# Layer 2 of a four-layer network: the order of a turn's links, and one product instruction for each half

## The chip, the cores and the metric

The kernel runs on one core of a Trainium2 chip. What counts is the device time of one launch in microseconds. A core has five engines that each work through their own queue in order: TensorE (PE in the profile), VectorE (DVE), ScalarE (ACT), GpSimd (POOL) and SyncE (SP), which here issues every DMA. They wait for each other through semaphores.

## The reference

A batch of 16 images of 64 x 64 pixels and 256 channels, all float32, goes through four residual layers. Each computes `x = x + layer(group_norm(x))`. Cut to what matters:

```python
def _gn(v, G=32, eps=1e-5):        # mean and variance over all pixels and the 8 channels of a group
    ...
# layer 0: linear attention, ends in a norm over channels
x = x + _L0_conv_ref(_gn(x), ...)
# layer 1: channel gate, a scan and a 7x7 gate, batch norm, relu
x = x + _L1_conv_ref(_gn(x), ...)
# layer 2: involution 3x3
x = x + _L2_conv_ref(_gn(x), ...)
# layer 3: involution 7x7
x = x + _L3_conv_ref(_gn(x), ...)

def _L2_conv_ref(x, Wr, br, gamma, beta, mean, var, Ws, bs, Wi, bi):
    r = relu(((x @ Wr + br) - mean) * rsqrt(var + 1e-3) * gamma + beta)
    w = (r @ Ws + bs).reshape(B, H, W, 16, 9)[:, :, :, :, None, :]   # 9 factors for each of 16 groups
    xi = x @ Wi + bi
    patches = stack(the 9 shifted copies of xi, padded).reshape(B, H, W, 16, 16, 9)
    return sum(w * patches, -1).reshape(B, H, W, 256)
```

Note the last reshape: the nine shifted copies of 256 channels stand one behind the other as 2304 numbers, which are cut into 256 runs of nine. So an output channel is a sum over nine neighbours in that row of 2304, each multiplied by a factor.

## The kernel before

The program has stages, one behind the other: layer 0 with the statistics for layer 1; a short stage for the scan and the gates; one long loop for the end of layer 1, all of layer 2, and the preparation of layer 3; then layer 3. The change lies in the long loop, in `for n in range(TURNS)`. Its order is written out by hand (`tc.manual_schedule()`): each engine gets its instructions in the order of the text.

**A turn** handles 512 pixels (8 rows, one `rc`; eight turns make an image) of up to four jobs at once, which are `LAG` turns apart, so that each works on an older chunk:

- *the end of layer 1* (`end_of_layer1`, lag 0), in three parts that the loop starts with `next(ending)`. First, on VectorE, two links that scale the loaded x1: `z` and `pf` (L975; the second is written over its own factor, so the profile calls it pf). Then, on ScalarE, the relu of both (L981) and, on GpSimd, the sums with x1 that make x2 (L985). Last, on ScalarE, the squares of x2 for the group norm of layer 2 (L992).
- *the projection of layer 2* (`projected`, lag 12): TensorE multiplies x2 by `Wi` (px, L1038) and ScalarE writes it into the padded image `pad` (L1042).
- *the involution* (lag 20). One turn ahead, `prepare` makes r (pr and rt, L1059 and L1062), the transposed patches `xs` (36 transposes L1084 into nine PSUM tiles pt, nine copies L1088 by ScalarE) and the factors `pw` (L1069). In the turn itself, `residual` transposes x2 into the PSUM tiles `lo`, one for each half of 128 output channels (L1100). `products` multiplies patches by factors on VectorE (pd, L1107), four instructions of 1152 elements for each half. The nine products of an output are summed for half 0 on GpSimd (`sums_on_pool`, L1122 and L1123) and for half 1 on VectorE (a reduce, L1258). The residual `lo` is added to each half on VectorE (L1261, half 1 first). The result x3 is held in `made`; in the next turn `turned` transposes it back (L1135) and ScalarE evicts it as c3 (L1136) with the sums for the group norm of layer 3, and `statistics3` squares it (L1156).
- *the centring for layer 3* (`centred`, lag 30): GpSimd subtracts the group means from x3, loaded again as `xc`, into `cen` (L880), and twelve stores write it as `strips`.

**Norm links.** The group norms are generators with small instructions on 128 x 2 elements. `begun` starts them with a fill (L113 to L123); `step()` moves every running one on by a link: a matmul (L134), a copy (L140), a deviation of three instructions (L146 to L148), a second matmul (L151), the inverse square root (L93, L94). `step()` stands three times in a turn: behind `turned`, behind the products, and at the end behind the residual. Each image has two such norms, for layers 2 and 3.

**DMAs.** SP issues all of them in the order of the text. A turn begins with the loads for the next one (x2p, x2r, x1 as two, pf as two), then come the stores that the turn before left in `stores`, in the order in which its jobs put them there (L1215), then the four loads of xc. Each is issued with one of eight semaphores, taken in turn.

**Buffers.** The PSUM pool `tr` has three tiles that pr, pt, px and the norms' matmuls share in turn; `pw` has three, `lo` two (one a half). In SBUF, xs, pd, x1, x2, c3, xc and cen have two each, x2r and x3 three.

Of the kernel before, what the change touches and what calls it, by code (L numbers as in the profile page):

```python
# [11 lines left out]
ALU = mybir.AluOpType  # L12
# [3 lines left out]
P = 128  # L16
C = 256
# [19 lines left out]
def network(ctx: ExitStack, tc: tile.TileContext, a: dict, out: bass.AP):  # L37
    nc = tc.nc
# [59 lines left out]
    def step():  # L98

        for c in list(chains):  # L100
            if next(c, c) is c:
                chains.remove(c)
# [77 lines left out]
    with ExitStack() as st:  # L180
# [366 lines left out]
        def loads(n):  # L547
            for job in jobs(n):
                if job[0] == "q":
                    load("xn", job[1], job[3])  # L550
                else:
                    load(*job)
# [78 lines left out]
    with ExitStack() as st:  # L631
# [57 lines left out]
        for n in range(10):  # L689
            delta, c = n // 2, n % 2  # L690
# [28 lines left out]
        with tc.manual_schedule():  # L719
# [25 lines left out]
            for n, (ch, g) in enumerate(steps):  # L745
# [18 lines left out]
                b, k = g * 8, min(8, NI - g * 8)  # L764
# [134 lines left out]
    with ExitStack() as st:  # L899
# [45 lines left out]
        def taken(name):  # L945

            n = [k for k, _ in loaded].index(name)
            return loaded.pop(n)[1]
# [11 lines left out]
        def load_centred(i, rc):  # L960
            load("xc", [P, 4, C], *(
                (lambda t, k=k: t[:, k], src) for k, src in enumerate(centred_from(i, rc))
            ))

        def end_of_layer1(i, rc):

            if rc == 0:
                st0[i] = [
                    wk.tile([P, 2, NCH], F32, tag=f"st0{k}", name="st0") for k in range(2)
                ]  # L970
            sums, squares = st0[i]
            x1, pf = taken("x1"), taken("pf")
            zs = [wk.tile([P, 2, 256], F32, tag="z", name="z", bufs=1), pf]
            for h, z in enumerate(zs):
                nc.vector.scalar_tensor_tensor(  # L975
                    z, x1[:, h], ngm1[:, i, h : h + 1], pf, ALU.add, ALU.mult
                )
            yield
            x2 = wk.tile([P, 2, CT], F32, tag="x2", name="x2")
            for h, z in enumerate(zs):  # L980
                nc.scalar.activation(  # L981
                    z, z, AF.Relu, bias=bnp[:, 1, h : h + 1], scale=ab[:, 0, i, h : h + 1],
                    accum_out=sums[:, h, rc : rc + 1],
                )
                nc.gpsimd.tensor_tensor(  # L985
                    x2[:, h].rearrange("p (t g) -> p g t", g=2), z, x1[:, h], ALU.add
                )
            stores.append((x2_d[i, rc], x2))
            yield
            sq = wk.tile([P, CT], F32, tag="sq", name="sq", bufs=1)  # L990
            for h in range(2):
                nc.scalar.activation(  # L992
                    sq, x2[:, h], AF.Square,
                    bias=ngm1[:, i, h : h + 1], accum_out=squares[:, h, rc : rc + 1],
                )
            if rc == NCH - 1:
                begun.append(norm2(i))
# [104 lines left out]

        def products(oh, pw, xs):
            pd = pd_p.tile([P, 4, P, 9], F32, tag="pd", name="pd")
            for r in range(4):
                run = xs[:, r : r + 3].rearrange("p e j c -> p (e j c)")
                nc.vector.tensor_tensor(  # L1107
                    pd[:, r].rearrange("p (g f) k -> p g f k", f=16),
                    run[:, oh * 9 * P : (oh + 1) * 9 * P].rearrange(
                        "p (g f k) -> p g f k", f=16, k=9  # L1110
                    ),
                    pw[:, r].rearrange("p (g k) -> p g k", k=9).unsqueeze(2).broadcast_to(
                        [P, 8, 16, 9]
                    ),
                    ALU.mult,
                )
            return pd

        def sums_on_pool(pd, x3):
# [5 lines left out]
        def turned(i, rc, x3):  # L1125

            if rc == 0:
                st3[i] = [
                    wk.tile([P, 2, NCH], F32, tag=f"st3{k}", name="st3") for k in range(2)
                ]  # L1130
            c3 = wk.tile([P, 2, 2, 256], F32, tag="c3", name="c3", bufs=2)
            for oh in range(2):
                pt = tr.tile([P, 4, P], F32, tag="tr", name="pt")
                for r in range(4):
                    nc.tensor.transpose(pt[:, r, :], x3[:, r, oh * P : (oh + 1) * P], ident)  # L1135
                nc.scalar.activation(  # L1136
                    c3[:, oh], pt.rearrange("p r t -> p (r t)").rearrange("p (t g) -> p g t", g=2),
                    AF.Copy, accum_out=st3[i][0][:, oh, rc : rc + 1],
                )
            x3n = x3_d[i].rearrange("(g r w) c -> g w r c", g=2, w=HW)  # L1140
            for g in range(2):
                stores.append((x3n[g][:, rc * 4 : rc * 4 + 4], x3[g:P:2]))
            for h in range(2):
                stores.append((
                    c3_d[i, :, h].rearrange("p (g t) -> p g t", g=2)[
                        :, :, rc * 256 : rc * 256 + 256
                    ],
                    c3[:, h],
                ))
            return c3  # L1150
# [23 lines left out]
        def centred(i, rc):  # L1174
            cen = wk.tile([P, 4, 4, 64], F32, tag="cen", name="cen")
            stores.extend(centred_strips(i, rc, taken("xc"), cen, gmb[i]))
# [6 lines left out]

        LAG = (0, 12, 20, 30)
        TURNS = NI * NCH + 23

        def jobs(n):

            at = [divmod(n - lag, NCH) for lag in LAG]
            return [
# [13 lines left out]
        with tc.manual_schedule():  # L1206
            loads(0)
            ahead, made = None, None
            for n in range(TURNS):
                end, proj, inv, cen = jobs(n)  # L1210
                nxt = jobs(n + 1)[2]
                done, stores[:] = list(stores), []
                loads(n + 1)
                for dst, src in done:
                    nc.sync.dma_start(out=dst, in_=src)  # L1215
                nxt_cen = jobs(n + 1)[3]
                if nxt_cen:
                    load_centred(*nxt_cen)
                now, ahead = ahead, None
                for c in begun:  # L1220
                    next(c)
                chains.extend(begun)
                begun.clear()
                ending = end_of_layer1(*end) if end else None
                if ending:
                    next(ending)
                if inv:
                    w1 = weights(now[1], 1)
                    x3 = wk.tile([P, 4, C], F32, tag="x3", name="x3", bufs=3)

                def prepare():
                    x2r, rt = reduced2(*nxt)
                    ahead = [x2r, rt]
                    ahead.append(patches(*nxt, lambda: ahead.append(weights(rt, 0))))
                    return ahead

                if nxt and nxt[1]:
                    ahead = prepare()
                if ending:
                    next(ending)  # L1240
                if inv:
                    los = residual(now[0])
                c3 = turned(*made) if made else None
                step()
                if proj:
                    projected(*proj)
                if inv:
                    pd = products(0, now[2], now[3])
                    sums_on_pool(pd, x3)
                if nxt and not nxt[1]:  # L1250
                    ahead = prepare()
                if inv:
                    pd1 = products(1, w1, now[3])
                step()
                if made:
                    statistics3(*made[:2], c3)
                if inv:
                    nc.vector.tensor_reduce(x3[:, :, P:C], pd1, AX.X, ALU.add)  # L1258
                    for oh in (1, 0):
                        half = x3[:, :, oh * P : (oh + 1) * P]  # L1260
                        nc.vector.tensor_tensor(half, half, los[oh], ALU.add)  # L1261
                step()
                if ending:
                    next(ending, None)
                made = (*inv, x3) if inv else None
                if cen:
                    centred(*cen)
            for dst, src in stores:
                nc.sync.dma_start(out=dst, in_=src)

# [2 lines left out]
    with ExitStack() as st:  # L1273
# [203 lines left out]
        for n, (i, quarter, t) in enumerate(turns):  # L1477
# [41 lines left out]
            if n % gap == 2 and n // gap < NCH:  # L1519
                cen = wk.tile([P, 4, 4, 64], F32, tag="xw", name="cen", bufs=6)  # L1520
# [3 lines left out]
            if n in features:  # L1524
                tp, k = features[n]
# [124 lines left out]
```

## Time and profile before

| What | Value |
|---|---|
| Median of the runs shown | 8503.4 us (8499.9 to 8507.17, three runs) |
| The profiled execution | 8500.31 us, span 8498.4 us |
| Long loop, first z to last reduce | 3428 to 6105 us of the span |
| First product of the long loop | 3562 us |
| Busy in the span | PE 81%, DVE 72%, ACT 57%, POOL 36% |
| DMA over the span | 1695.70 MB, mean 200 GB/s |
| Granted TensorE clock | 0.908 |

The page of the profile has six parts: busy time of each engine, the span in 40 slices of 212 us, the DMA queues, the chain that ended last, the groups of instructions, and the DMA issues. A group's row gives line, engine, operation and tiles (out<-in), the count, and behind the bar the busy time in us and the mean length of one in ns; behind the second bar stands the idle time of the engine just before these instructions, and what ended it. In a timeline, the columns are the start in us, the length in us (of all that are merged in the row), engine, line and tiles. The word DMA with a tile means that a transfer ended the wait. Of SP the profile shows the issues; a row's length is the time to issue, not to land.

### The profile page before, as it was taken

Reading aid. Unit: us, or ns where it says so; the run is one execution under the profiler, and the core shown is the slowest. Engines: PE = TensorE matmul, PEld = TensorE weight load, DVE = VectorE, ACT = ScalarE, POOL = GpSimd, SP = SyncE. Lnnn points to the kernel's source line nnn. Section 1 sums busy time; section 2 is a strip of 40 time slices with the busy share of each in tenths; the row PEclk is TensorE's granted clock in tenths of the full one; section 3 lists DMA queues with packets and bytes.
Section 4 is the critical chain, followed back from the end, with each engine's and each line's share of the span. In section 5 each row is a group of like instructions: output and inputs, shape, how many; then the busy total and the mean of one; then the engine's idle time right before and its main releaser. Section 6 shows DMA issues by size and latency. Waiting matters only on the chain. (4 is left out here: it accounts for less than half of the span.)

```text
span 8498.4 us, 215779 instructions
## 1 busy us (share of the span) xinstructions
PE 6860.2 (81%) x88348; PEld 5148.9 (61%) x88348; DVE 6094.1 (72%) x7839; ACT 4825.8 (57%) x11136; POOL 3041.0 (36%) x2154
## 2 busy tenths in 40 slices
PE   7888888888888776577777777778588888888888
PEld 5666666666666641255555555555476767777777
DVE  6777787777777757499999999999744444444444
ACT  3555555555555437666666666665355555555555
POOL 1222222222222100467777777777511111211112
PEclk9999999999999869799888888889699999999999
DMA  6644434434333228657767767766578888888887
GB/s 223 188 138 137 137 134 147 139 129 137 131 118 109 100 69 284 221 194 241 234 228 238 236 230 238 237 232 202 174 223 256 253 246 252 254 260 260 257 252 243
DMA packets 1081774, 1695.70 MB, mean 200 GB/s; under 512 B 138833, under 2 KB 684962, under 8 KB 1079634
## 3 DMA queue, kind: packets, MB, share of 16 engines
q1 hardware_dynamic: 1080786, 1681.90, 61.0%
q8 instruction: 696, 11.40, 0.6%
q14 instruction: 292, 2.39, 0.1%
HBM read 1234.54 MB, written 469.76 MB: 201 GB/s over the span
## 5 line engine op out<-in xcount | busy, mean ns | idle before, releaser
L1107 DVE TENSOR_TENSOR pd<-xs,pw 128x1152 f32<-128x1152 f32 x1024 | 1305.3, 1347 | 5.2 <-ACT xs L1088 5.2
L1367 PE MATMUL pk<-rt,span 64*128 64x176 f32 x12288 | 1182.8, 329 | 44.7 <-issue 41.4
L1122 POOL TENSOR_TENSOR pd<-pd 128x2048 f32<-128x2048 f32 (+2 forms) x384 | 1067.7, 2780 | 313.0 <-DVE pd L1107 293.0
L1377 ACT ACTIVATE wm<-pk,spanb 128x176 f32<-128x176 f32 x2560 | 846.0, 424 | 553.9 <-PE pk L1367 550.7
L1453 POOL TENSOR_TENSOR ex<-ex,rx 128x192 f32<-128x192 f32 (+2 forms) x768 | 437.2, 570 | 1852.4 <-DVE ex L1446 1403.2
L1367 PEld LDWEIGHTS pk<-rt,span 64*128 64x128 f32 x12288 | 973.1, 192 | 119.3 <-issue 64.9
L1446 DVE SCALAR_TENSOR_TENSOR ex<-pa,msk,ex 128x192 f32<-128x192 f32 x704 | 294.2, 418 | 1045.2 <-ACT ex L1445 991.3
L292 PE MATMUL pkv<-wq,xn 128*128 128x256 f32 x4096 | 967.6, 382 | 16.0 <-ACT va L301 16.0
L1433 PE MATMUL pa<-wm,xw 126*32 126x48 f32 x45056 | 756.6, 215 | 215.3 <-issue 198.9
L375 POOL TENSOR_TENSOR qa<-qa,mq 128x1024 f32<-128x1024 f32 x256 | 507.2, 2004 | 1177.0 <-DVE mq L387 469.7
L1382 DVE TENSOR_TENSOR wm<-pk,spanb 128x704 f32<-128x704 f32 x896 | 793.8, 888 | 182.8 <-PE pk L1367 180.1
L292 PEld LDWEIGHTS pkv<-wq,xn 128*128 128x128 f32 x4096 | 770.8, 192 | 228.7 <-issue 101.4
L1433 PEld LDWEIGHTS pa<-wm,xw 126*32 126x32 f32 x45056 | 625.5, 112 | 404.0 <-issue 356.5
L1038 PE MATMUL px<-x2p,wis 128*128 128x512 f32 x1024 | 588.4, 724 | 194.3 <-ACT c L1136 125.1
L1084 PE MATMUL pt<-ident,pad 128*128 128x128 f32 x4608 | 618.1, 288 | 121.9 <-ACT rt L1062 83.3
L1084 PEld LDWEIGHTS pt<-ident,pad 128*128 128x128 f32 x4608 | 528.1, 148 | 276.6 <-ACT rt L1062 104.6
L1088 ACT COPY xs<-pt 128x512 f32<-128x512 f32 x1152 | 592.8, 601 | 135.7 <-PE pt L1084 125.6
L1258 DVE TENSOR_REDUCE x<-pd 128x512 f32<-128x4608 f32 x128 | 633.5, 4949 | 1.9
L280 PE MATMUL pq<-xn,wq 128*128 128x512 f32 x1024 | 528.8, 632 | 89.3 <-DVE xn L166 70.8
L423 PE MATMUL py<-wo,o 128*128 128x256 f32 x2048 | 529.4, 415 | 33.0 <-DVE maps L510 30.1
L423 PEld LDWEIGHTS py<-wo,o 128*128 128x128 f32 x2048 | 490.8, 311 | 67.0 <-issue 41.0
L1445 ACT ACTIVATE ex<-pa,msk 128x192 f32<-128x192 f32 x704 | 299.4, 425 | 399.3 <-PE pa L1433 201.4
(233 smaller groups left out, 11871.5 us busy)
## 6 DMA issues: line engine op xcount, KB each, us to landing
xw<-strips SPq DMA_DIRECT2D x1408, 256.0 KB
xn<-in_x SPq DMA_DIRECT2D x256, 512.0 KB
x_d<-x SPq DMA_DIRECT2D x256, 512.0 KB
xin<-in_x SPq DMA_DIRECT2D x128, 512.0 KB
x<-in_x SPq DMA_DIRECT2D x128, 512.0 KB
xm<-x_d SPq DMA_DIRECT2D x128, 512.0 KB
x<-x_d SPq DMA_DIRECT2D x128, 512.0 KB
x<-x_d SPq DMA_DIRECT2D x256, 256.0 KB
```

Source lines behind the costliest of these rows:

```text
L292: nc.tensor.matmul(pkv[:, q], lhsT=xn[:, h, q * P : (q + 1) * P], rhs=wq[:, h, f0 + P : f0 + 384], start=(h == 0), stop=(h == 1),)
L423: nc.tensor.matmul(py[:, q, :], lhsT=om[i, hf][:, :, ch * 4 + q], rhs=wo[:, hf, :], start=(hf == 0), stop=(hf == 1),)
L1038: nc.tensor.matmul(px, lhsT=w[:, h, fh * P : (fh + 1) * P], rhs=x2[:, h], start=(h == 0), stop=(h == 1),)
L1084: nc.tensor.transpose(pt[:, k, h * P : (h + 1) * P], lines[:, h, rc * 4 + e + k, 2 * j : 2 * j + P], ident,)
L1088: nc.scalar.copy(xs[:, e : e + 2, j, :], pt)
L1107: nc.vector.tensor_tensor(pd[:, r].rearrange("p (g f) k -> p g f k", f=16), run[:, oh * 9 * P : (oh + 1) * 9 * P].rearrange("p (g f k) -> ...
L1122: nc.gpsimd.tensor_tensor(pd[..., 0:n], pd[..., 0:n], pd[..., n : 2 * n], ALU.add)
L1258: nc.vector.tensor_reduce(x3[:, :, P:C], pd1, AX.X, ALU.add)
L1367: nc.tensor.matmul(pkv[:, b, m], lhsT=span[half, first + gg, s0 : s0 + P], rhs=rto[half, o // 4 * 2 + m, :], start=True, stop=True,)
L1377: nc.scalar.activation(dst[:, m // 2, m % 2], pkv[:, m // 2, m % 2], AF.Identity, bias=spanb[:, g0 + m : g0 + m + 1],)
L1382: nc.vector.tensor_tensor(dst, pkv, spanb[:, g0 : g0 + 4].rearrange("p (b m) -> p b m", b=2).unsqueeze(3).broadcast_to([P, 2, 2, NTL]), AL ...
L1433: nc.tensor.matmul(pav[p0 : p0 + 32, :, tj * TC : (tj + 1) * TC].rearrange("c g (w v) -> c g w v", v=2), lhsT=xw[0:TILE_IN, k, tj, 32 * q ...
```

## The change

In `products`, the four instructions of a half become one on 4608 elements, with an address pattern of one more level (the four rows overlap in `xs`, so the pattern is written out with `bass.AP`). The order of a turn changes: z, pf, the relus, the x2 sums and the centring come first; then the step of the running norms and the start of new ones; then the residual of half 0 of the turn before, which `made` now carries along with its `lo` tile. The step that stood at the turn's end is now this one at the front; the other two stay behind `turned` and behind the products. The residual of half 1 stays behind the reduce. The squares of x2 stay at the end. The centring's lag becomes 31, since it moves from the end of a turn to the front. In SP's queue the stores of the turn before thus have the order x2, strips, x3, c3, in place of x2, x3, c3, strips. All instructions but the products are the same, and as many as before.

```diff
@@ products
             pd = pd_p.tile([P, 4, P, 9], F32, tag="pd", name="pd")
-            for r in range(4):
-                run = xs[:, r : r + 3].rearrange("p e j c -> p (e j c)")
-                nc.vector.tensor_tensor(
-                    pd[:, r].rearrange("p (g f) k -> p g f k", f=16),
-                    run[:, oh * 9 * P : (oh + 1) * 9 * P].rearrange(
-                        "p (g f k) -> p g f k", f=16, k=9
-                    ),
-                    pw[:, r].rearrange("p (g k) -> p g k", k=9).unsqueeze(2).broadcast_to(
-                        [P, 8, 16, 9]
-                    ),
-                    ALU.mult,
-                )
+            run = xs.rearrange("p e j c -> p (e j c)")[:, oh * 9 * P : (oh + 1) * 9 * P]
+            run = bass.AP(run.tensor, run.offset, [run.ap[0], [3 * C, 4], [9 * 16, 8], [9, 16], [1, 9]])
+            nc.vector.tensor_tensor(
+                pd.rearrange("p r (g f) k -> p r g f k", f=16),
+                run,
+                pw.rearrange("p r (g k) -> p r g k", k=9).unsqueeze(3).broadcast_to(
+                    [P, 4, 8, 16, 9]
+                ),
+                ALU.mult,
+            )
             return pd
@@ the long loop
-        LAG = (0, 12, 20, 30)
+        LAG = (0, 12, 20, 31)
...
                 now, ahead = ahead, None
+                ending = end_of_layer1(*end) if end else None
+                if ending:
+                    next(ending)
+                    next(ending)
+                if cen:
+                    centred(*cen)
+                step()
                 for c in begun:
                     next(c)
                 chains.extend(begun)
                 begun.clear()
-                ending = end_of_layer1(*end) if end else None
-                if ending:
-                    next(ending)
+                if made:
+                    half = made[2][:, :, 0:P]
+                    nc.vector.tensor_tensor(half, half, made[3], ALU.add)
...
                 if nxt and nxt[1]:
                     ahead = prepare()
-                if ending:
-                    next(ending)
                 if inv:
                     los = residual(now[0])
-                c3 = turned(*made) if made else None
+                c3 = turned(*made[:3]) if made else None
                 step()
...
                 if inv:
                     nc.vector.tensor_reduce(x3[:, :, P:C], pd1, AX.X, ALU.add)
-                    for oh in (1, 0):
-                        half = x3[:, :, oh * P : (oh + 1) * P]
-                        nc.vector.tensor_tensor(half, half, los[oh], ALU.add)
-                step()
+                    half = x3[:, :, P:C]
+                    nc.vector.tensor_tensor(half, half, los[1], ALU.add)
                 if ending:
                     next(ending, None)
-                made = (*inv, x3) if inv else None
-                if cen:
-                    centred(*cen)
+                made = (*inv, x3, los[0]) if inv else None
```

## The prediction

> **What bounds the kernel now.** I read the page first: part 2 for the stage, part 5 for its groups.
>
> ```profile
> DVE  6777787777777757499999999999744444444444
> ...
> L1107 DVE TENSOR_TENSOR pd<-xs,pw 128x1152 f32<-128x1152 f32 x1024 | 1305.3, 1347 | 5.2 <-ACT xs L1088 5.2
> ...
> L1258 DVE TENSOR_REDUCE x<-pd 128x512 f32<-128x4608 f32 x128 | 633.5, 4949 | 1.9
> ```
>
> VectorE is at nine tenths only in slices 17 to 27, about 3600 to 6100 us: the involution of layer 2, 128 turns. A gain must come from there. In the timeline, reduce starts are 5959.69 and 5976.18 where layer 1 has ended: 16.49 us a turn, which is eight products (10.2), the reduce (4.98) and two residual adds (1.31), with no gap. With layer 1 in the turn and no centring yet, turns take 17.94 (reduces at 3614.49 and 3632.43): two links z and pf add 1.46. But in the long middle, eight turns take 5609.33 - 5445.47 = 163.9, or 20.48 each. So 2.5 us a turn are lost there. The groups of the stretch 3785 to 5772 us, shapes apart, tell where:
>
> ```profile
> L975 DVE SCALAR_TENSOR_TENSOR z<-x,ngm,pf 128x512 f32<-128x512 f32 x96 | 139.8, 1456 | 2.0 <-DMA x<-x_d 0.4
> ...
> L1261 DVE TENSOR_TENSOR x<-x,lo 128x512 f32<-128x512 f32 x194 | 126.7, 685 | 79.6 <-POOL x L1123 73.7
> ...
> L985 POOL TENSOR_TENSOR x<-z,x 128x512 f32<-128x512 f32 x96 | 122.8, 1280 | 326.2 <-ACT z L981 242.3 <-DMA c_d<-c 55.0 <-DMA x<-x_d 19.8
> ...
> L975 DVE SCALAR_TENSOR_TENSOR pf<-x,ngm,pf 128x512 f32<-128x512 f32 x96 | 72.2, 752 | 3.4
> ```
>
> z takes 1456 ns where the same operation on pf takes 752; the residual add of half 0 waits 73.7 us for GpSimd's sums. The timeline shows both causes in one turn:
>
> ```profile
> 5673.12 2.36 POOL L880 TENSOR_TENSOR cen<-xc,gmb 128x1024 f32<-128x1024 f32 x1
> ...
> 5674.14 1.90 DVE L975 SCALAR_TENSOR_TENSOR z<-x,ngm,pf 128x512 f32<-128x512 f32 x1
> ...
> 5680.11 3.03 ACT L1088 COPY xs<-pt 128x512 f32<-128x512 f32 x6 [0.60 <-PE pt L1084]
> ...
> 5682.97 0.87 ACT L981 ACTIVATE z<-z,bnp,ab 128x512 f32<-128x512 f32 x1
> ...
> 5684.01 1.28 POOL L985 TENSOR_TENSOR x<-z,x 128x512 f32<-128x512 f32 x1 [8.52 <-DMA c_d<-c]
> ...
> 5696.77 0.69 DVE L1261 TENSOR_TENSOR x<-x,lo 128x512 f32<-128x512 f32 x1 [4.04 <-POOL x L1123]
> ```
>
> z is stretched while GpSimd's centring runs. Its relu then stands in ScalarE's queue behind the nine patch copies, which are late; GpSimd's x2 adds wait for the relu, the sums of half 0 wait behind the adds (one queue), and VectorE pays 4.04 us.
>
> The second reading is SP's queue, where a turn begins with the load of x2p:
>
> ```profile
> 4441.90 0.40 SPq L942 DMA_DIRECT2D x2p<-x_d  x1
> ...
> 4445.83 2.84 SPq L1215 DMA_DIRECT2D x_d<-x  x3
> ...
> 4449.29 1.67 SPq L1215 DMA_DIRECT2D c_d<-c  x2
> ...
> 4451.05 8.67 SPq L1215 DMA_DIRECT2D strips<-cen  x12
> ...
> 4462.37 0.40 SPq L942 DMA_DIRECT2D x2p<-x_d  x1
> ```
>
> 20.47 us and hardly a gap: SP is as full as VectorE. Its 27 issues at their usual lengths, with the 0.045 between them, make 16.9. The other 3 to 3.5 are waits for landings (the queue's waits name DMA x2r, x2p, x and xc, 208 us in this stretch) and issues lengthened beside them. The program gives every DMA one of eight semaphores in turn, so an issue waits until the eighth before it has landed: the third store x_d could go at 4447.91, 6.0 after x2p.
>
> [...] The trace [...] shows what happens when GpSimd runs back to back (the ramp of layer 2):
>
> ```profile
> 3481.29 0.16 DVE L146 TENSOR_TENSOR gn_d<-gn_mv,gn_m 128x2 f32<-128x2 f32 x1
> ...
> 3481.47 1.27 POOL L985 TENSOR_TENSOR x<-z,x 128x512 f32<-128x512 f32 x1 [3.59 <-ACT z L981]
> 3481.49 1.27 DVE L147 TENSOR_TENSOR gn_d<-gn_d 128x2 f32<-128x2 f32 x1
> 3482.70 1.26 POOL L985 TENSOR_TENSOR x<-pf,x 128x512 f32<-128x512 f32 x1
> ...
> 3482.79 1.19 DVE L148 TENSOR_TENSOR gn_d<-gn_d,gn_mv 128x2 f32<-128x2 f32 x1
> ```
>
> Each tiny link loses one whole GpSimd instruction. Products and residual adds [...] keep their length beside GpSimd. [...]
>
> **The change, part by part**, for a turn that starts at T with z.
>
> *One product a half.* Four products start 1.275 apart, 1.2 of it the elements and 0.075 the fixed part. One of 4608 costs 4.8 + 0.075 = 4.875, two 9.75: 0.45 saved a turn. The address pattern gets one more level; the trace doesn't show such a one. If each of its steps cost the fixed part again, nothing would be saved, and twice that would lose 0.45; the elements lie in the same order as before, so I take the 0.45 saved and keep both ends. GpSimd's sums already waited for all four rows, so nothing starts later.
>
> *Relu, x2 adds and centring to the front.* z comes before the centring of its turn, so its excess goes: (1456-752) x 96 = 68 us. Is it blocked by the sums instead? They take 10.3 from the end of half 0's product; VectorE needs 4.9 + 5.0 + 0.65 = 10.55 to come to z. They just miss: 0 to 0.3 a turn, I take 0. ScalarE runs the relus 0.8 after T, GpSimd the adds at 1.77 and 3.0 and the centring at 4.3 to 6.7. Half 0's product ends at 1.46 + 0.65 + 4.9 = 7.0, so the sums start on time if the centring has its xc. The wait of 73.7 us for L1123 goes. ScalarE's other work, 12.75 a turn with the relus, ends near T+17, just inside the turn; the patch copies are now behind the relus but are needed a turn later, a cover of some 10 us.
>
> *Half 0's residual behind the links.* Same instruction, 0.65. The turned copies for layer 3 now need it at T+2.2; TensorE comes to them at about T+8, so it is hidden, and so is the lo buffer that it frees later; with that cover gone it would cost the 0.65 in each of 128 turns, 83 us.
>
> *Norm links behind z and pf.* They no longer meet the centring once (L118, L116 and both L146: 49 links of about 1.47 in place of 0.16 = 64 us in the stretch), but start at T+1.5 and run into three GpSimd instructions. A fill has four two-input links: the first slips in, the others end with the two adds and the centring, at 6.7 in place of 2.5: 4.2 lost. A deviation has three: about 1.05. With 25 fills and 24 deviations, 130 us: 66 more than now. Bounds: 0 (the adds come late) and 200.
>
> VectorE's sum for the stretch of 97 turns: -44 -68 -74 +66 = -120, i.e. 19.25 a turn.
>
> *SP.* Nothing is added, but the order in a turn becomes loads, x2, strips, x3 twice, c3 twice, xc: the stores of x3 and c3 pass behind the strips, when DMA is quiet. The wait of the eighth after x2p stays (it becomes the second strip: eight issues take 4.0 against 6.0 to land); what followed it, x2r to c_d, is partly covered by strips of 0.7 each. On the other side x2p now follows the first x3 store by eight issues, 4.9 us, against about 5 for such a store (the second c_d of the turn shown, issued at 4450.16, has its last semaphore update at 4455.20). So 2.5 to 3.2 of waits in place of 3.3: 19.4 to 20.1 a turn, bounds 18.5 and 21.5. SP, not VectorE, is then the later one: I take 19.75. The gain is (20.48-19.75) x 97 = 71 us.
>
> *The rest.* The 20 turns after layer 1 give 0.45 each, 9; the 11 before the first centring have no strips and two of them wait like the one shown: 0.45 x 11 plus 3 = 8. The lag of 31 adds a set of twelve strips at the end (11 us of SP), but each centring is a turn's end earlier: +3.
>
> Sum: -71 -9 -8 +3 = -85, against 8500.31 for the profiled execution (span 8498.4), which is 3 below the median: 8503.4 - 85 = 8418, say **8420**.
>
> **Rivals.**
> *VectorE alone bounds* (0.24). If SP's waits fall below 2.3, the turn is 19.25, or less if GpSimd's adds miss the links: -120 to -150 in the stretch, in all 8340 to 8385. For it: SP's bare issues are 16.9. Against: landings of 6 us with eight semaphores.
> *SP doesn't move* (0.14). The turn stays at 20.2 to 20.5 whatever VectorE saves; the tail and the start remain: 8480 to 8500. For it: the same 27 issues and 4.8 MB.
> *SP gets slower* (0.11). Fifteen short issues, from x3 to x2, now stand in one row, and x2p and x2r wait for stores. If these land after more than some 5.5 us, the waits rise to 4 and above and SP's turn to 21; and since the centring now stands ahead of the sums in GpSimd's queue, a late xc stops the sums and through them z. 21 x 97 is 50 more than now, minus 17: 8535. It decides above 20.65 a turn.
> *The long product is slower than four* by its pattern: each 0.1 us costs 26 us if VectorE bounds; I give it no case of its own.
>
> **How the numbers follow.** Likeliest (0.51) is the SP-bound turn of 19.4 to 20.1, 8385 to 8455. The range 8345 to 8500 takes in that, most of the first rival and the second. A measurement here tells some 0.2%, 17 us, from no change: faster 0.82 (the first two cases and half of the third), same 0.07, slower 0.11.
>
> **What would show it.** The products' group: x256 at about 4950 ns, or the pattern costs. z's mean at 752, or the sums block it. L985 waiting 1 us for ACT z, at T+1.77, in every turn. L147, L148, L121 to L123 with means near 1 us. L1231 without a wait for POOL. SP's queue gapless at 19.4 to 20.1 says it bounds; gaps before x2p (waiting for PE px) say VectorE does. I am wrong if the reduces are more than 20.5 apart, or if the centring waits for xc and the product waits behind it.

## The result, and the profile after

The changed kernel takes 8439.5 us, the median of 4 runs (8433.6 to 8440.9), against 8505.3 for the kernel before on the same chip: a ratio of 0.9916, interval 0.9897 to 0.9935, so 66 us less. On another chip, later, the ratio was 0.9942 (0.9929 to 0.9955), 52 us less. The gain is real and smaller than the 85 us foretold.

The page of the changed kernel, its two groups of the products and the reduce:

```profile
L1107 DVE TENSOR_TENSOR pd<-xs,pw 128x4608 f32<-128x4608 f32 x256 | 1255.8, 4946 | 42.2 <-ACT xs L1088 42.2
...
L1261 DVE TENSOR_REDUCE x<-pd 128x512 f32<-128x4608 f32 x128 | 633.4, 4949 | 2.2 <-DVE gm L140 0.3
```

The long product takes 4946 ns, the reduce over as many elements 4949: the extra address level has no cost that shows. The page's slices of VectorE look nearly as before. So I cut each profiled execution at the starts of the same reduces; a "middle turn" is the mean over the 96 turns from the 12th reduce to the 108th. The last reduce starts at 6095.5 us before (not 6105, as the table of the kernel before has it) and at 6033.1 after.

| stretch, us | before | after | difference | predicted |
|---|---|---|---|---|
| up to the first z (not touched) | 3428.0 | 3419.3 | -8.7 | 0 |
| first z to 12th reduce | 357.1 | 345.2 | -11.9 | -8 |
| 96 middle turns | 1965.7 (20.48 each) | 1934.0 (20.15 each) | -31.7 | -71 |
| last 20 turns | 344.6 | 334.6 | -10.0 | -9 |
| last reduce to the end | 2402.9 | 2404.5 | +1.6 | +3 |
| span | 8498.4 | 8437.5 | -60.9 | -85 |

The first row is not the change: in all thirteen profiles of this study that part ran from 3407 to 3438 us. The shortfall lies in the middle. There the groups of VectorE (first fence) and of GpSimd (second), from 3765 to 5698 us, shapes apart, read:

```profile
L975 DVE SCALAR_TENSOR_TENSOR pf<-x,ngm,pf 128x512 f32<-128x512 f32 x96 | 115.5, 1204 | 3.4
L975 DVE SCALAR_TENSOR_TENSOR z<-x,ngm,pf 128x512 f32<-128x512 f32 x96 | 112.6, 1173 | 0.0
...
L1231 DVE TENSOR_TENSOR x<-x,lo 128x512 f32<-128x512 f32 x96 | 65.2, 679 | 10.8 <-POOL x L1121 10.8
L148 DVE TENSOR_TENSOR gn_d<-gn_d,gn_mv 128x2 f32<-128x2 f32 x24 | 15.5, 644 | 0.8
```

```profile
L880 POOL TENSOR_TENSOR cen<-xc,gmb 128x1024 f32<-128x1024 f32 x96 | 227.6, 2371 | 141.0 <-DMA xc<-x_d 37.9 <-DMA x2p<-x_d 35.1 <-issue 35.0
...
L985 POOL TENSOR_TENSOR x<-z,x 128x512 f32<-128x512 f32 x96 | 123.4, 1285 | 299.8 <-ACT z L981 206.4 <-DMA x<-x_d 37.5 <-DMA x2r<-x_d 25.9
```

The wait for GpSimd's sums is down from 73.7 to 10.8. But z has only come from 1456 to 1173 ns, and pf has risen from 752 to 1204: both are still blocked, now by the sums. Without the sums beside them z takes 744 to 747 ns and pf 750 to 753 (25 and 57 of the 96 turns), beside the sums 1323 and 1864 in the mean. (Before, z took 750 to 754 in the 48 turns without the centring beside it and 1771 to 2683 in the other 48.) By the timeline of the 96 turns, the sums start over 0.5 us after the end of half 0's product in 69 of them. In 48 of these the centring ahead of the sums has waited for its data (141 us in all 96 turns); in the other 21 it has not, and x2's adds ahead of it came late. Here is a turn of each kind, late adds first (VectorE and GpSimd rows of the timeline):

```profile
4818.84 9.82 DVE L1107 TENSOR_TENSOR pd<-xs,pw 128x4608 f32<-128x4608 f32 x2 [3.36 <-ACT xs L1088]
...
4823.53 1.28 POOL L985 TENSOR_TENSOR x<-z,x 128x512 f32<-128x512 f32 x1 [8.78 <-DMA x<-x_d]
...
4826.00 2.37 POOL L880 TENSOR_TENSOR cen<-xc,gmb 128x1024 f32<-128x1024 f32 x1
4828.32 8.82 POOL L1120 TENSOR_TENSOR pd<-pd 128x2048 f32<-128x2048 f32 x3
...
4834.35 1.59 DVE L975 SCALAR_TENSOR_TENSOR z<-x,ngm,pf 128x512 f32<-128x512 f32 x1
```

```profile
4957.40 9.80 DVE L1107 TENSOR_TENSOR pd<-xs,pw 128x4608 f32<-128x4608 f32 x2
...
4963.07 2.36 POOL L880 TENSOR_TENSOR cen<-xc,gmb 128x1024 f32<-128x1024 f32 x1 [2.57 <-DMA xc<-x_d]
4965.38 8.48 POOL L1120 TENSOR_TENSOR pd<-pd 128x2048 f32<-128x2048 f32 x3
...
4972.96 1.44 DVE L975 SCALAR_TENSOR_TENSOR z<-x,ngm,pf 128x512 f32<-128x512 f32 x1
...
4974.44 2.04 DVE L975 SCALAR_TENSOR_TENSOR pf<-x,ngm,pf 128x512 f32<-128x512 f32 x1
```

In the first, half 0's product is done at 4823.79, its sums start at 4828.32, and z runs into them. The wait of 8.78 is put down to a DMA; the relu that the add needs ran only at 4822.56, behind ScalarE's four squares. In the second the centring itself waits 2.57 us for xc, and the sums start some 3 us after half 0's product.

Does SP still set the pace? Its queue, one turn:

```profile
4615.43 0.40 SPq L942 DMA_DIRECT2D x2p<-x_d  x1
...
4620.22 9.58 SPq L1213 DMA_DIRECT2D strips<-cen  x12
...
4632.45 2.87 SPq L942 DMA_DIRECT2D xc<-x_d  x4
4635.42 0.40 SPq L942 DMA_DIRECT2D x2p<-x_d  x1
```

19.99 us, in which SP's longest idle gap is 0.61. But ScalarE and TensorE also wait for each other in a ring (relus, rt, patches, px, pads, squares, next relus): TensorE waits 236 us for rt here, ScalarE 353 for px. And VectorE is busy for 1831 of the 1945 us from 3785 to 5730. Three candidates, then: **SP's issues**, **the ring of ScalarE and TensorE**, **VectorE** with what blocks it. In the trace SP's own instructions take 16.5 us of the 20.15 and its waits 3.06; that SP is the bound here, the next runs show.

### The profile page after: what moved, and what is told of

Read it like the earlier page. It is cut to its first block, busy times and chain, and to the rows that moved or that the text cites. A ratio compares the mean times of both kernels' runs of the same rounds, so it can differ in the third digit from the quotient of the medians.

```text
span 8437.5 us, 214993 instructions
## 1 busy us (share of the span) xinstructions
PE 6919.5 (82%) x88348; PEld 5293.7 (63%) x88348; DVE 6026.7 (71%) x7071; ACT 4858.5 (58%) x11136; POOL 3065.7 (36%) x2154
## 4 chain that ended last, share of the span: by engine, by line
PE 49%; DVE 19%; DMA 11%; ACT 9%; issue 7%; SPq 3%; POOL 2%; DVEq 0%; ACTq 0%; POOLq 0%
PE pk L1366 13%; PE pa L1432 8%; PE pkv L292 4%; PE pt L1084 4%; PE px L1038 4%; DMA x<-x_d 3%; DVE pd L1107 3%; PE py L423 2%; PE pq L280 2%; DMA xn<-in_x 2%; PE pctx L350 2%; PE pr L1333 2%; ACT sq L432 1%; DVE mq L387 1%; DVE x L451 1%
## 5 line engine op out<-in xcount | busy, mean ns | idle before, releaser
L1107 DVE TENSOR_TENSOR pd<-xs,pw 128x4608 f32<-128x4608 f32 x256 | 1255.8, 4946 | 42.2 <-ACT xs L1088 42.2
L1084 PE MATMUL pt<-ident,pad 128*128 128x128 f32 x4608 | 756.3, 330 | 266.7 <-ACT rt L1062 266.7
L1084 PEld LDWEIGHTS pt<-ident,pad 128*128 128x128 f32 x4608 | 673.9, 175 | 407.2 <-ACT rt L1062 292.6
L1088 ACT COPY xs<-pt 128x512 f32<-128x512 f32 x1152 | 619.4, 591 | 239.4 <-PE pt L1084 233.8
L1261 DVE TENSOR_REDUCE x<-pd 128x512 f32<-128x4608 f32 x128 | 633.4, 4949 | 2.2 <-DVE gm L140 0.3
L1038 PE MATMUL px<-x2p,wis 128*128 128x512 f32 x1024 | 519.3, 653 | 111.8 <-issue 63.8
```

The source lines that it names most:

```text
L1038: nc.tensor.matmul(px, lhsT=w[:, h, fh * P : (fh + 1) * P], rhs=x2[:, h], start=(h == 0), stop=(h == 1),)
L1084: nc.tensor.transpose(pt[:, k, h * P : (h + 1) * P], lines[:, h, rc * 4 + e + k, 2 * j : 2 * j + P], ident,)
L1107: nc.vector.tensor_tensor(pd.rearrange("p r (g f) k -> p r g f k", f=16), run, pw.rearrange("p r (g k) -> p r g k", k=9).unsqueeze(3).broa ...
```

## The experiments

Middle turns are from the profiled execution of each; ratios are against the kernel before on the same chip.

### Which of the three sets the turn

**Fewer transfers.** In layer 2 the eight narrow strip stores of a turn go; once an image, a turn or more later, the same columns are copied from strips to strips, one transfer a turn. SP issues 20 transfers a turn, not 27.

```diff
@@ centred_strips (called here with sides=False)
-            for u0, u1, w0, dt in ((0, TC, 3, 0), (TC - 3, TC, 0, 1), (0, 3, TC + 3, -1)):
+            for u0, u1, w0, dt in ((0, TC, 3, 0), (TC - 3, TC, 0, 1), (0, 3, TC + 3, -1))[: 3 if sides else 1]:
...
@@ sides_of, called after the last centring of an image
+                (strips[i, q, 3:67, w0 : w0 + 3, t0 : t0 + NTC - 1, :].rearrange("r w t c -> r w (t c)"),
+                 strips[i, q, 3:67, w1 : w1 + 3, t1 : t1 + NTC - 1, :].rearrange("r w t c -> r w (t c)"))
+                for q in range(4) for w0, t0, w1, t1 in ((0, 1, TC, 0), (TC + 3, 0, 3, 1))
...
@@ the long loop
-                done, stores[:] = list(stores), []
+                done, stores[:] = copies[:1] + list(stores), []
...
```

> The changed kernel with fewer transfers issued: the eight narrow strip stores of each turn (three columns to the left and right of every tile) are replaced by copies from the strips to the strips once an image, one a turn, so that SP issues 20 transfers a turn in place of 27. If SP's queue sets the turn of 20.05 us, it loses some 4 us of issues and the turn falls to what VectorE needs, about 19.2: 80 us less, 8360. If the loop between ScalarE and TensorE sets it (relus, rt, patches and px on TensorE, pads, squares, next relus), the turn stays at 19.8 to 20.1: 8415 to 8440. If VectorE, with its z and pf blocked by GpSimd's sums, sets it, also 8420 to 8440.

Measured: 8318.8 us, ratio 0.977 (0.9753 to 0.9786); middle turn 18.64. SP's queue, one turn of it:

```profile
4622.83 0.33 SPq L942 DMA_DIRECT2D x2p<-x_d  x1
...
4625.74 0.61 SPq L1224 DMA_DIRECT2D strips<-strips  x1
...
4627.08 3.45 SPq L1224 DMA_DIRECT2D strips<-cen  x4
...
4635.13 2.56 SPq L942 DMA_DIRECT2D xc<-x_d  x4
4643.01 0.33 SPq L942 DMA_DIRECT2D x2p<-x_d  x1
```

SP now idles from 4637.69 to 4643.01, waiting for px: 3.38 us a turn over the 96 turns. The groups of VectorE from 3769 to 5558 us (L1242 is L1231 of the changed kernel):

```profile
L975 DVE SCALAR_TENSOR_TENSOR z<-x,ngm,pf 128x512 f32<-128x512 f32 x96 | 83.4, 869 | 0.0
L975 DVE SCALAR_TENSOR_TENSOR pf<-x,ngm,pf 128x512 f32<-128x512 f32 x96 | 80.3, 836 | 3.4
...
L1242 DVE TENSOR_TENSOR x<-x,lo 128x512 f32<-128x512 f32 x96 | 65.3, 681 | 0.0
...
L148 DVE TENSOR_TENSOR gn_d<-gn_d,gn_mv 128x2 f32<-128x2 f32 x24 | 3.9, 161 | 0.8
```

It beats both kernels, and by more than expected (1.5 us a turn in place of 0.9): the centring no longer waits for its data, so the sums mostly end in time, z and pf are nearly free, and of the norm links only L116 still takes long (694 ns; L148 takes 161). The bytes are not the reason: from 3790 to 5550 us the changed kernel moves 239 GB/s x 20.15 = 4.8 MB a turn, this one 257 x 18.64 = 4.8. What fell is the time in SP's own instructions: 16.5 us of a turn in the changed kernel and 12.7 here, while the queue's waits for anything but px are 2.9 in both.

**Short squares**, for the ring:

```diff
-                    sq, x2[:, h], AF.Square,
+                    sq[:, 0:32], x2[:, h, 0:32], AF.Square, scale=8.0,
...
-                    sq, c3[:, oh].rearrange("p g t -> p (g t)"), AF.Square,
+                    sq[:, 0:32], c3[:, oh, 0, 0:32], AF.Square, scale=8.0,
```

> The changed kernel in which the four squares that ScalarE makes in each turn (the second moments of x2 and of c3) run over 32 elements in place of 512, scaled up; the variances are thereby wrong, everything else is done. ScalarE loses about 4 x 0.5 = 2 us a turn. If the serial loop between ScalarE and TensorE sets the turn, the relus and rt come 2 us earlier in each turn, TensorE waits less for rt, the sums of half 0 end earlier and z is no longer blocked: the turn falls to about 19.2, the total to some 8360. If SP's queue sets the turn, it stays at 20.05, 8435 to 8440.

Measured: 8454.1, ratio 0.9925 (0.9907 to 0.9942); middle turn 20.11. A square takes 320 ns in place of 720, so 1.6 us are off ScalarE's turn, and the pace stays. With SP full, the ring is no bound.

**Four products again**, with SP full and with SP relieved:

```diff
-            run = xs.rearrange("p e j c -> p (e j c)")[:, oh * 9 * P : (oh + 1) * 9 * P]
...
+            for r in range(4):
+                run = xs[:, r : r + 3].rearrange("p e j c -> p (e j c)")
...
```

> The changed kernel with four product instructions a half again; the new order alone. If VectorE sets the changed turn of 20.05 us, the turn grows by 0.45 and the total by about 57 us, to 8497. If SP's queue or the loop between ScalarE and TensorE sets it, only the start and the tail lose: about 14 us, 8453.

Measured: 8463.5, ratio 0.9933 (0.9914 to 0.9952); middle turn 19.98, no longer than with one product.

> The changed kernel with fewer transfers, and four product instructions a half. If VectorE sets the turn of 18.64 there, it pays the whole 0.45 a turn: 19.1 in the middle, +57 in all, 8376. If something else has become the bound (TensorE and ScalarE's loop), less than half of that.

Measured: 8389.3, ratio 0.9843 (0.9822 to 0.9864), against 0.977 with one product, on another chip. Middle turn 19.20 against 18.64, so 0.56 more, where 0.45 was expected. Of these 54 us over the 96 turns the products take 37 (43 were expected); most of the rest is in norm links that now meet GpSimd's work (L148 takes 689 ns in place of 161). So VectorE sets the turn as soon as SP is relieved, and not before.

### What each part of the change is worth

**One product alone**, in the kernel before:

> The kernel before with one product instruction a half and nothing else of the change. The bare saving is two times 0.23 us in each of 128 turns. If VectorE alone sets the turn of the kernel before, all of it shows: about 57 us, 8448. If SP's queue sets the long middle (20.48 us a turn without a gap), only the start and the tail gain: about 14 us, 8491. If the serial loop between ScalarE and TensorE sets it, also about 14 us, 8491.

Measured: 8492.6, ratio 0.997 (0.996 to 0.9981), so 16 to 34 us, more than the 14 expected; but its middle turn is 20.49, as before. The profiled execution lies only 7 us below that of before in span, its tail 6.5. The groups of VectorE from 3780 to 5747 us say where the saving in the middle went:

```profile
L975 DVE SCALAR_TENSOR_TENSOR z<-x,ngm,pf 128x512 f32<-128x512 f32 x96 | 148.4, 1546 | 2.0 <-DMA x<-x_d 0.4
L1259 DVE TENSOR_TENSOR x<-x,lo 128x512 f32<-128x512 f32 x192 | 125.4, 685 | 101.5 <-POOL x L1121 95.7
```

The shorter products are given back as a longer wait for GpSimd's sums (95.7) and a longer z (1546).

**The kernel before with fewer transfers**: the same cut of SP, without the change.

> The kernel before with the fewer transfers (the narrow strip stores replaced by one copy a turn, 20 issues in place of 27), so that SP no longer bounds: what is the reordering and the one product worth when VectorE sets the turn? By the prediction's VectorE sum (products 0.45, z 0.7, wait for the sums 0.77, links 0.68 the other way) the turn is 1.2 us above the 18.64 of the changed kernel with fewer transfers: 19.9, and 8440. If the late z and the wait for the sums were only consequences of SP being late, they go with it, and only the product's 0.45 and the links' collisions remain: 19.1 to 19.3, 8375.

Measured: 8474.2, ratio 0.9947 (0.9926 to 0.9968); middle turn 20.16. Its groups of VectorE from 3781 to 5716 us:

```profile
L975 DVE SCALAR_TENSOR_TENSOR z<-x,ngm,pf 128x512 f32<-128x512 f32 x96 | 141.1, 1469 | 2.0 <-DMA x_d<-x 0.4
L1272 DVE TENSOR_TENSOR x<-x,lo 128x512 f32<-128x512 f32 x192 | 124.7, 685 | 48.1 <-POOL x L1123 42.3
...
L116 DVE TENSOR_SCALAR gn_mv<-mom 128x2 f32<-128x2 f32 x12 | 18.1, 1505 | 0.0
```

z beside the centring, the wait for the sums and the blocked links are all still there with SP relieved, so they belong to the old order and not to SP. The kernel before had two bounds that nearly met: VectorE at 20.16 a turn and SP at 20.48. The cut alone brings 0.5%, the change alone 0.6 to 0.8%, both together 2.3%. With SP relieved the change is worth 8474 - 8319 = 155 us (on two chips; 151 by the two ratios), 1.52 a middle turn.

**SP's order of stores.** In the changed kernel, the old order again; in the kernel before, the new order alone. In both the strips are first collected in a list of their own, `strip_stores`:

```diff
@@ changed kernel
-                done, stores[:] = list(stores), []
+                done, stores[:] = stores + strip_stores, []
@@ kernel before
-                done, stores[:] = list(stores), []
+                done, stores[:] = stores[:1] + strip_stores + stores[1:], []
```

> The changed kernel with SP's old order within a turn: the stores of x3 and c3 ahead of the strips again; nothing else moves. If the place of the x3 and c3 stores behind the strips is what took 0.33 us from the turn (SP's gaps before x3 fell by 0.8 and those before the strips rose by 1.0), the turn goes back to about 20.5 and the total to some 8470. If the gain came from the engines' reordering, the turn stays at 20.0 to 20.15, 8435.

Measured: 8476.0, ratio 0.9944 (0.9924 to 0.9963); middle turn 20.30: between the two cases, so it was run again beside the changed kernel.

> The changed kernel unaltered, so that the two below can be held against it on one chip: 0.9916 of before as measured already, some 20.1 us a turn in the middle.

Measured: 8458.6, ratio 0.9942 (0.9929 to 0.9955); middle turn 20.13.

> The changed kernel with SP's old order of stores, once more, in more rounds, since 20.30 us a turn against 20.15 and 19.98 in two kernels with the new order is within what one profile shows. If the place of the stores matters by itself, it is slower than the changed kernel by 0.2 to 0.4% (15 to 30 us); if not, the two agree within 0.1%.

Measured: 8464.3, ratio 0.9947 (0.9935 to 0.9959); middle turn 20.23. The intervals overlap nearly whole. By the profiles the order of the stores is worth 0.10 us a turn in this pair, and 0.15 in the first (20.30 against 20.15), not the 0.33 by which the change shortens the turn.

> The kernel before with SP's new order of stores alone: x2, then the strips, then x3 and c3; the four products and every engine's order as before. If SP's order of stores is what moved the turn of a queue that bounds, its turn falls from 20.48 to about 20.15 and the total by some 30 us, to 0.9965 of before. If SP needed the engines' new order too (the centring a turn's end earlier, so that the first strip store finds its data and slots free), it stays at 20.4 to 20.5, within 0.1% of before.

Measured: 8638.5, ratio 1.0157 (1.014 to 1.0174), slower by more than either case expected; middle turn 21.85. SP's waits from 3798 to 5896 us (total us, times, longest):

```profile
SPq L1216 <- POOL cen L880: 136.3, 50, 8.1
SPq L942 <- PE px L1038: 123.0, 41, 4.8
```

In the old order the centring is GpSimd's last work, so a strip store that goes first waits for it, and everything queued on SP behind it waits too. The new order of stores is harmless only because the centring went to the front with it.

### Trying to go further

With fewer transfers TensorE still waits 229 us for rt, so rt was put ahead of the relus. GpSimd's adds and centring move behind it in the text with them, and so behind the step that stands at the front of a turn:

```diff
                     x2r, rt = reduced2(*nxt)
+                    if ending and nxt[1]:
+                        next(ending)
+                    if cen and nxt[1]:
+                        centred(*cen)
...
```

> The changed kernel with fewer transfers, and rt's activation ahead of the two relus in ScalarE's queue, so that TensorE isn't held (it waits 230 us for rt there). If VectorE alone sets the turn, TensorE's wait is free and the x2 adds only come 0.8 us later: 18.6 to 18.9 a turn, 8315 to 8345. If the loop between ScalarE and TensorE is close behind, the turn falls by 0.1 to 0.3, 8290 to 8310.

Measured: 8378.7, ratio 0.9832 (0.9805 to 0.9858): slower than with the relus first; middle turn 19.40. TensorE's wait for rt falls to 85 us, but VectorE pays. A turn of its timeline, and one of its groups from 3759 to 5622 us:

```profile
4708.24 1.21 DVE L121 TENSOR_TENSOR mom<-gn_mv,ngm 128x2 f32<-128x2 f32 x1
4709.49 1.21 DVE L122 TENSOR_TENSOR mom<-mom 128x2 f32<-128x2 f32 x1
4710.73 2.28 DVE L123 SCALAR_TENSOR_TENSOR gn_mv<-mom 128x2 f32<-128x2 f32 x1
```

```profile
L123 DVE SCALAR_TENSOR_TENSOR gn_mv<-mom 128x2 f32<-128x2 f32 x24 | 37.8, 1573 | 0.8
```

Three links, 0.16 us long with the relus first, take 1.21, 1.21 and 2.28: by their lengths they lose one GpSimd instruction each, two adds (1.28 in the changed kernel) and the centring (2.37 there). Over the 96 turns VectorE's small instructions are busy 98 us longer than with the relus first, and wait 42 less for their inputs; z and pf, longer by 10, and 6 of waiting for xs bring this to the 74 us that the middle has lost. This is the collision that the prediction feared for the change itself.

## Why the prediction was right, and where it was off

**What bounds** was right: SP, not VectorE, takes the later place after the change. The cut in issues shows it; with SP relieved, VectorE bounds, as the four products show. The turn of 20.15 lies just above the 19.4 to 20.1 of the likeliest case. The total falls inside that case's 8385 to 8455, near its upper end, and some luck helped there: the part that the change doesn't touch was 8.7 us shorter in this profile, and the start gained 4 more than foretold.

**VectorE's sum** was right in kind and somewhat small: 1.24 us a turn predicted, 1.52 measured with SP relieved (20.16 to 18.64). That it came so near is partly luck, since its terms missed in both directions. By the timelines of the two kernels with fewer transfers, over 96 turns, the products gave 37 us (44 foretold), z and pf together 55 (68), the residual's wait 44 (74), and the links with the waits before them gave 10 where they were to take 66. With SP full it hardly shows: over the 96 turns VectorE spends 145 us more than with SP relieved, 64 of them inside z and pf, 37 in waits for xs and the rest at the links and the residual.

**SP's term was the mis-sized one.** The step reads "2.5 to 3.2 of waits in place of 3.3 ... I take 19.75". By its own measure (the turn less 16.9 of bare issues) the kernel before stood at 3.58 and the changed one at 3.25: 0.33 less, where taking 19.75 assumed 0.73. That is 0.4 x 96 = 38 us, and the middle turns are 39 short. Its ground, that x3 and c3 stores pass behind the strips, when DMA is quiet (in the turn that it shows, 114 GB/s from 4457 to 4462 us and 374 from 4446 to 4451), failed: the gaps ahead of the x3 stores fell from 1.12 to 0.33 us a turn and those ahead of SP's separate semaphore instructions from 1.39 to 0.90, but those ahead of the strips rose from 0.75 to 1.78, since the first strips now wait for the loads of xc, x2p and x2r. SP's longest waits of the changed kernel from 3765 to 5698 us (total us, times, longest) show it; before, the stores' longest were 62.2 for x2r, 52.9 for x2p, 47.6 for x and 45.5 for xc:

```profile
SPq L1213 <- DMA xc<-x_d: 71.6, 123, 1.2
SPq L1213 <- DMA x2p<-x_d: 56.6, 93, 1.6
SPq L1213 <- DMA x2r<-x_d: 56.5, 95, 1.6
```

The waits moved; putting the stores back changes the turn by 0.10 to 0.15. What did help is less settled: of SP's waits, 3.37 us a turn before and 3.06 after, those for px fell from 0.24 to 0.12 and those for GpSimd from 0.15 to 0.08, in both orders of stores. I read this as two bounds that no longer meet, but no run separates it further.

**z at 752** was wrong (1173, and pf 1204). The text named the way ("or the sums block it") but took none of it, because it assumed that the centring finds xc and that x2's adds start 1.77 us after the turn does. The centring waited 141 us, and the adds start 4.9 us after z in the mean. With fewer transfers the centring waits none, the adds start 3.4 after z, and z falls to 869.

**The links' loss** (130 us of new collisions taken, bounds 0 and 200) came out near the lower bound. From before to after, the links that met the centring (L116, L118 and both L146) fell from 70.7 to 17.2 us, and L121 to L123, L147 and L148 rose only from 19.5 to 37.1. What rose instead is the wait of VectorE's small instructions for ScalarE and TensorE, from 4 to 55 us. The reason given for that bound, adds that come late, holds: x2's adds waited 206 us for the relus, 2.15 a turn and not 1. ScalarE did not come "just inside the turn": its squares of one turn run into the relus of the next. That cost nothing with SP full, as the short squares show, and even spared the links, as rt first shows.

**The products** run at the predicted pace (4946 against 4875 + 75). The split of 1.275 into 1.2 and 0.075 was an estimate: within a half, starts lie 1.265 us apart for 1152 elements before, and from half to half 4.865 for 4608 after, which gives 1.2 for the elements (1.04 ns each) and 0.065 besides. So the saving is 0.39 a turn and not 0.45. Beside GpSimd the products kept their length: before, from 3785 to 5751 us, all lie between 1342 and 1351 ns, 596 of the 768 at least partly beside its work, and the residual adds, all beside it, between 678 and 690; why they do and z does not, no run shows. The last 20 turns gained 10.0 where 9 was foretold.

**The rival of SP getting slower** did not come, but half of its mechanism did: a late xc holds up the centring, the sums and through them z. With it came the first half of a sign of being wrong, "if the centring waits for xc"; the second half, "and the product waits behind it", did not: the products wait 37 us in the middle, for xs. The turn did not become longer, since SP's 20.15 leaves VectorE room: with SP relieved, its work fits in 18.64. The turn of 21.85 with the strips first in the kernel before has another cause, which no rival named: the stores wait for the centring.

## What to carry to other kernels

Count the issues of a DMA queue that is always busy before tuning the engines beside it: here 7 fewer of 27 transfers a turn, with the same bytes, brought 0.5% without the reordering and 1.5 to 1.7% on top of it, and only then did the reordering pay in full. When two bounds nearly meet, test each with the other relieved, since each part alone looks nearly worthless. A store moved ahead in a queue needs its producer moved ahead too: without that, it cost 1.37 us a turn here.

## What was not expected of the hardware

A copy of 64 x 3 runs of 1792 bytes from DRAM to DRAM takes SP 0.61 us to issue, no more than one strip store (12 of them take 8.1), and only SP waited for its landing, 2.9 us in the 96 middle turns. One product of 4608 elements in place of four of 1152 shortens VectorE's busy time by 0.19 us (with fewer transfers, 980.4 us for 769 products and 947.0 for 193), a little less than the 0.23 foretold; its overlapping pattern of one more level has no price that the trace shows.
